# The last 1x1 convolution of a C2f-attention block by one step of Strassen's scheme, and the softmax sums issued one product earlier

## The chip, the cores and the metric

The kernel runs on one core of one Trainium2 chip. Times are device microseconds (us) of an execution. TensorE is called PE in the profile, VectorE DVE, ScalarE ACT; SP and POOL are the two engines that issue the transfers that matter here, each on its own queue (SPq, POOLq).

## The reference

```python
B, C1, C2, N, F, HEADS = 8, 512, 512, 2, 32, 4        # 8 images, 512 channels, 32x32 pixels; C = 256
def L0(x):                                            # on group-normalised x
    t = cbs(x, cv1_w, cv1_bn, 0)                      # 1x1 conv, batch norm, SiLU
    ys = [t[:, :C], t[:, C:]]
    for i in range(N):
        yi = ys[-1]
        z = cbs(yi, m_cv1_w[i], m_cv1_bn[i], 1)       # 3x3 convolution
        z = bot_attention(z, m_qkv_w[i], m_rw[i], m_rh[i])
        z = silu(bn_eval(conv2d(z, m_cv2_w[i], 0), m_cv2_bn[i]))   # "m2" in the kernel
        ys.append(yi + z)
    return cbs(concatenate(ys, axis=1), cv2_w, cv2_bn, 0)          # cv2: 1024 -> 512 channels
out = x + L0(group_norm(x))
```

For one image cv2 is a product of a 512 x 1024 matrix (weights) with a 1024 x 1024 one (channels by pixels). Everything is float32.

## The kernel before

One program handles the eight images in a row. The parts that matter: cv2, the loop of the attention, and what stands around both.

```python
def cv2(b, w2, ys, begun=None, parts={}):
    def residual(oc, half):                            # 256 KB of x, by the POOL queue
        t = act.tile([P, HALF], F32, tag="xr", name="x_res", bufs=2)
        nc.gpsimd.dma_start(t, rows_of(x, oc, half))
        return t
    pieces = [(oc, half) for oc in range(NO) for half in range(NH)]
    res = [residual(*pieces[0]), residual(*pieces[1])]
    for i, (oc, half) in enumerate(pieces):
        if half == 0:
            ...                                        # ps = 16 matmuls of this output chunk
        t = act.tile([P, HALF], F32, tag="t", name="t", bufs=2)
        silu(t, ps[:, half, :], bn_cv2 + oc)           # ScalarE
        nc.vector.tensor_tensor(t, t, res.pop(0), ALU.add)
        q.dma_start(rows_of(out, oc, half), t)         # q is the POOL queue
        if i + 2 < len(pieces):
            res.append(residual(*pieces[i + 2]))

for i in range(len(pairs) + 1):                        # the attention: logits one step ahead of v
    ...
    if i > 0:
        times_v(pairs[i - 1])
        g, j0 = pairs[i - 1][0]
        if j0 == 0:
            if g > 0:
                s_drams[g - 1] = sums(g - 1)
            with tc.issue_after(added.ins):
                behind.get(g, lambda: None)()          # loads, or work for PE's gaps

xs = [load_x(act, b + 1, c, NX) for c in range(NX)]    # at the start of image b: x of the next, by the SP queue
```

The softmax sums of a group of heads go through DRAM: `sums` writes a row (`s_dram`), it comes back over 128 partitions (`sums_all`), VectorE takes reciprocals (`rc`), these are written (`r_dram`) and broadcast (`rs`), all by the SP queue. VectorE multiplies `ao` by `rs` one group later.

## Time and profile before

| | before |
|---|---|
| median of 3 runs | 2486.34 us |
| span of the profiled run | 2485.1 us |
| PE busy | 2416.4 us, 97% |
| DVE, ACT busy | 60%, 38% |

The lines that carry the bound are in the prediction.

The whole idle time before a row goes to what came last. Take cv2 of the second image, whose PE rows the prediction shows. (The prediction calls it the fourth; the rows follow the fourth m2 of the trace, and each image has two.) There ScalarE is idle for 13.81 us up to the SiLU at 662.95, but PE ended the matmuls of that output chunk only near 660.5 (656.93 + 3.60), so some 2.4 us of it are the output's. Seven rows like this, of 13.8 us each, make up nearly all of the 104.8. The next two pairs of outputs (SiLU at 674.30 and 688.03) are 13.73 us apart, and none of their SiLUs waits for a transfer.

### The profile page before, as it was taken

How to read it: one execution, taken by the hardware profiler on the slowest of the kernel's cores; microseconds unless marked ns; L12 is line 12 of the kernel's file. 1: busy time of each engine (PE TensorE's matmuls, PEld its weight loads, DVE VectorE, ACT ScalarE, POOL GpSimd, SP SyncE). 2: the span in 40 equal slices, each digit the busy share in tenths (PEclk: the TensorE clock that was granted, in tenths of full speed). 3: DMA queues.
4: the chain of work that ended last, by engine and by line, in shares of the span. 5: the costliest groups of instructions: out<-in, count | busy, mean ns of one | idle time of the engine just before them, and what ended most of it. 6: DMA issues, size and time to landing. Idle time of an engine off the chain costs nothing.

```text
span 2485.1 us, 35553 instructions
## 1 busy us (share of the span) xinstructions
PE 2416.4 (97%) x14626; PEld 1198.2 (48%) x14626; DVE 1488.6 (60%) x2482; ACT 939.7 (38%) x1280; POOL 104.9 (4%) x355
## 2 busy tenths in 40 slices
PE   6799999999999999999999999999999999999998
PEld 4436446363463634636355363644536354363533
DVE  7678554766456664666546665566564665636654
ACT  2353522525134251443414334153431525325252
POOL 1000000000100001000010000100001000010001
PEclk9899999999999999999999999999999999999999
DMA  7124014040140402304032030502205021050102
GB/s 235 61 90 157 27 39 170 14 153 10 60 149 15 152 15 85 119 14 153 14 133 76 29 134 15 181 28 77 91 10 203 10 87 43 22 191 14 69 10 65
DMA packets 82203, 200.01 MB, mean 80 GB/s; under 512 B 27889, under 2 KB 37809, under 8 KB 69745
## 3 DMA queue, kind: packets, MB, share of 16 engines
q1 hardware_dynamic: 68080, 152.00, 17.8%
q0 software_dynamic: 11808, 45.62, 5.2%
q8 instruction: 117, 1.92, 0.3%
q14 instruction: 54, 0.43, 0.1%
q10 hardware_dynamic: 2144, 0.03, 0.0%
HBM read 167.74 MB, written 29.88 MB: 80 GB/s over the span
## 4 chain that ended last, share of the span: by engine, by line
PE 86%; DVE 5%; ACT 3%; issue 2%; DMA 0%; POOL 0%; SPq 0%; ACTq 0%; DVEq 0%
PE ps L266 33%; PE av_ps L505 15%; PE l_ps L479 14%; PE c_ps L695 13%; PE v_ps L445 4%; PE m_ps L716 4%; ACT pt L483 3%; PE s_ps L523 1%; DVE ao L513 1%; PE s_ps L541 1%; ACT t L252 1%; DVE acc L491 0%; DVE acc L489 0%; DVE v_in L325 0%; DVE st L368 0%
## 5 line engine op out<-in xcount | busy, mean ns | idle before, releaser
L483 ACT ACTIVATE pt<-l_ps 128x1024 f32<-128x1024 f32 x512 | 495.1, 1023 | 230.7 <-PE l_ps L479 230.7
L491 DVE TENSOR_TENSOR acc<-acc,pt 128x1024 f32<-128x1024 f32 x384 | 469.6, 1223 | 131.8 <-ACT pt L483 108.1
L479 PE MATMUL l_ps<-q,kr 64*64 64x512 f32 x4096 | 488.0, 594 | 8.5 <-ACT pt L483 8.5
L505 PE MATMUL av_ps<-pt,vT 64*64 64x512 f32 x4096 | 486.4, 592 | 9.0 <-DVE ao L513 7.5
L695 PEld LDWEIGHTS c_ps<-v_in,u 128*128 128x128 f32 x2688 | 302.6, 192 | 11.5 <-issue 6.7
L695 PE MATMUL c_ps<-v_in,u 128*128 128x128 f32 x2688 | 303.2, 275 | 4.2 <-DVE v_in L325 4.2
L505 PEld LDWEIGHTS av_ps<-pt,vT 64*64 64x64 f32 x4096 | 153.3, 133 | 306.1 <-issue 222.1
L479 PEld LDWEIGHTS l_ps<-q,kr 64*64 64x64 f32 x4096 | 150.2, 133 | 283.1 <-issue 259.1
L266 PE MATMUL ps<-x,w 128*128 128x512 f32 x512 | 227.8, 601 | 2.2 <-DVE x L401 2.2
L266 PE MATMUL ps<-z,qkv_sb 128*128 128x512 f32 x512 | 229.3, 595 | 0.4
L266 PE MATMUL ps<-ypad,w 128*128 128x512 f32 x512 | 227.8, 594 | 0.6 <-ACT t L252 0.6
L489 DVE TENSOR_TENSOR acc<-pt 128x1024 f32<-128x1024 f32 x64 | 78.4, 1225 | 136.8 <-ACT pt L483 136.8
L266 PEld LDWEIGHTS ps<-x,w 128*128 128x128 f32 x512 | 97.1, 192 | 130.8 <-issue 127.3
L266 PEld LDWEIGHTS ps<-ypad,w 128*128 128x128 f32 x512 | 96.5, 190 | 126.0 <-issue 124.6
L433 DVE TENSOR_TENSOR kr<-ps,rw_sb 128x512 f32<-128x512 f32 x64 | 41.2, 686 | 186.0 <-PE ps L266 186.0
L252 ACT ACTIVATE t<-ps,bh,sh 128x512 f32<-128x512 f32 x58 | 42.7, 775 | 274.6 <-PE ps L266 166.8
L266 PEld LDWEIGHTS ps<-z,qkv_sb 128*128 128x128 f32 x512 | 94.7, 190 | 107.2 <-issue 91.8
L778 DVE TENSOR_TENSOR t<-t,x_res 128x512 f32<-128x512 f32 x64 | 43.8, 690 | 170.2 <-ACT t L252 142.8
L266 PE MATMUL ps<-y,w 128*128 128x512 f32 x256 | 118.0, 599 | 4.1 <-ACT t L252 4.1
L332 ACT COPY m<-c_ps 128x256 f32<-128x256 f32 x96 | 35.5, 369 | 221.2 <-PE c_ps L695 214.7
L266 PE MATMUL ps<-ylast,w 128*128 128x512 f32 x256 | 117.2, 595 | 0.0
L445 PE MATMUL v_ps<-qkv_sb,z 128*128 128x256 f32 x512 | 115.7, 379 | 0.0
(121 smaller groups left out, 1980.9 us busy)
## 6 DMA issues: line engine op xcount, KB each, us to landing
u<-u SPq DMA_DIRECT2D x84, 1024.0 KB
w<-in_cv_w_dram SPq DMA_DIRECT2D x25, 1024.0 KB
x<-in_x_dram SPq DMA_DIRECT2D x32, 512.0 KB
x_res<-in_x_dram POOLq DMA_DIRECT2D x64, 256.0 KB, 3.8
out_dram<-t POOLq DMA_DIRECT2D x62, 256.0 KB, 2.9
u<-u_new POOLq DMA_DIRECT2D x12, 1024.0 KB, 5.4
rs<-r_dram SPq DMA_DIRECT2D x96, 128.0 KB
raw<-in_m_cv_w_dram SPq DMA_DIRECT2D x8, 576.0 KB
```

Source lines behind the costliest of these rows:

```text
L252: return nc.scalar.activation(dst, src, AF.Silu, scale=sh[:, k : k + 1], bias=bh[:, k : k + 1])
L266: nc.tensor.matmul(ps[:, half, :], w_of(k), rhs_of(k, half), start=(k == begin), stop=(k == end))
L433: nc.vector.tensor_tensor(dst, img(ps[:, half, :]), rw, ALU.add)
L445: nc.tensor.matmul(ps[:, at, :], z[:, k, ts(j0 + at, P)], qkv_sb[:, n, k, 2 * C : 3 * C], start=(k == 0), stop=(k == NM - 1),)
L479: nc.tensor.matmul(ps[kh * HD : (kh + 1) * HD, hd, :], kr[r, c, o : o + HD], q[r, c, ts(half, HALF)], start=True, stop=True,)
L483: exp = nc.scalar.activation(pt[:, i], ps, AF.Exp, scale=SCALE)
L489: return nc.vector.tensor_tensor(accs[g], pt[:, 0], pt[:, 1], ALU.add)
L491: ins = nc.vector.tensor_tensor(accs[g], accs[g], pt[:, i], ALU.add)
L505: nc.tensor.matmul(avs[g][hd * HD : (hd + 1) * HD, kh, :], vT[r, j, o : o + HD], pt[r, i, hd, :], start=(j == 0), stop=(j == NJ - 1),)
L695: nc.tensor.matmul(ps[:, row, col, :], us[i][:, k, row, col, :], vs[i][:, k, row, col, :], start=(k == 0), stop=(k == NM - 1),)
L716: nc.tensor.matmul(pss[oc][:, half, :], m2_sb[:, n, k, ts(oc, P)], ao[:, k, ts(half, HALF)], start=(k == 0), stop=(k == NM - 1),)
L778: nc.vector.tensor_tensor(t, t, res.pop(0), ALU.add)
```

## The change

The intent is to take an eighth of cv2's matmuls out in seven of the eight images (the last one keeps the plain form). Weights and inputs are cut in 2 x 2 blocks, and seven products of half size replace eight. The four sums of weight blocks are formed once, in the first image, written to DRAM and read back as `ws` in every image. VectorE forms the sums of inputs (`t_in`) and combines the products (`m1`, `c12`, `u3`, `m5`). Independently, the sums of the attention go ahead of the next group's first product with v.

```diff
+    def load_ws():                  # 4 MB of weight blocks and their sums, by the SP queue
+        ...
+    def make_ws(w2):                # first image only: 4 operations of VectorE, 2 MB written
+        ...
+        nc.vector.tensor_tensor(s1, a21, a22, ALU.add)
+        nc.vector.tensor_tensor(s2, s1, a11, ALU.subtract)
+        nc.vector.tensor_tensor(s3, a11, a21, ALU.subtract)
+        nc.vector.tensor_tensor(s4, a12, s2, ALU.subtract)
+        for w, dst in zip(sums, s_dram2):
+            nc.gpsimd.dma_start(dst, w)
 ...
                 if i > 0:
+                    g, j0 = pairs[i - 1][0]
+                    if j0 == 0 and g > 0:
+                        s_drams[g - 1] = sums(g - 1)
                     times_v(pairs[i - 1])
-                    g, j0 = pairs[i - 1][0]
                     if j0 == 0:
-                        if g > 0:
-                            s_drams[g - 1] = sums(g - 1)
                         with tc.issue_after(added.ins):
 ...
+        def strassen(b, ws, y0, y1):
+            ...                      # part1, part2: m1, m5 begun in the attention's tail, kept in SBUF
+            def spare(ps):
+                t = act.tile([P, 2, HALF], F32, tag="x", name="m_kept", bufs=NX)
+            ...
+            def finish(src):         # SiLU, residual, output, as in cv2: two buffers each
+                for o in range(2):
+                    oc, half = pieces.pop(0)
+                    t = act.tile([P, HALF], F32, tag="t", name="t", bufs=2)
+                    silu(t, src[:, o, :], bn_cv2 + oc)
+                    tt(t, t, res.pop(0), ALU.add)
+                    nc.gpsimd.dma_start(out[b, ts(oc, P), ts(half, HALF)], t)
+                    if len(pieces) >= 2:
+                        res.append(residual(*pieces[1]))
+            def part3(y2, ylast, last):
+                ...
+                finish(ps1)
+                tt(m1, new(s2, t2), m1, ALU.add)
+                c12 = spare(None)
+                tt(c12, ps5, m1, ALU.add)
+                finish(c12)
+                u3 = spare(None)
+                tt(u3, new(s3, t3), m1, ALU.add)
+                tt(m5, m5, u3, ALU.add)
+                finish(m5)
+                tt(u3, u3, new(a22, t4), ALU.subtract)
+                finish(u3)
 ...
+                if b == 0:
+                    make_ws(w2)
+                three = s.strassen(b, load_ws(), y0, y1)
                 for i in range(PAIRS):
                     us[0, i] = load_u(0, 0, i)
```

More of the change, by code (lines that the diff above doesn't have):

```diff
@@ L126, with block @@
     raws = [load_raw(0, 0, 0, "k")]
+    KB, CO = (2 + N) * NM // 2, C2 // 2
+    s_dram2 = [tc.dram_tile([P, 2, KB, CO], F32, name=f"s{i}") for i in range(2)]
+    def load_ws():
+        def block(o, i):
+            return cv2_w[ts(i, KB * P), ts(o, CO)].rearrange("(k p) o -> p k o", p=P)
+        pairs = (
+            (block(0, 0), s_dram2[0][:, 0]), (block(0, 1), s_dram2[0][:, 1]),
+            (s_dram2[1][:, 0], s_dram2[1][:, 1]), (block(1, 1),),
+        )
+        ws = []
+        for i, pair in enumerate(pairs):
+            w = ring([P, 2, KB, CO], f"ws{i}")
+            for j, src in enumerate(pair):
+                nc.sync.dma_start(w[:, j], src)
+                ws.append(w[:, j])
+        return ws
+    def make_ws(w2):
+        (a11, a21), (a12, a22) = ((w[:, :, :CO], w[:, :, CO:]) for w in w2)
+        sums = [ring([P, 2, KB, CO], f"s{i}") for i in range(2)]
+        s1, s4, s2, s3 = (w[:, j] for w in sums for j in range(2))
+        nc.vector.tensor_tensor(s1, a21, a22, ALU.add)
[4 more added lines that the diff above has]
+            nc.gpsimd.dma_start(dst, w)
     w1 = load_w1()
@@ L735, in cv2_products, with side, product @@
             return conv1x1(lambda k: w2[2 * k // nk][:, k % (nk // 2), ts(oc, P)], cat, nk, ks, ps, ends)
+        def side(y, half):
+            if len(y.shape) == 3:
+                return y[:, :, ts(half, HALF)]
+            return y[:, :, 1 + half * ROWS : 1 + (half + 1) * ROWS, :].rearrange("p c h w -> p c (h w)")
+        def product(ps, w, rhs, parts=(0, 1), onto=False):
+            for part in parts:
+                for o in range(2):
+                    for c in range(NM):
+                        k = part * NM + c
+                        nc.tensor.matmul(
+                            ps[:, o, :], w[:, k, ts(o, P)], rhs[part][:, c, :],
+                            start=(k == 0 and not onto), stop=(k == KB - 1),
+                            skip_group_check=onto,
+                        )
@@ new lines, in strassen, with sums_of, part1, part2 @@
+        def strassen(b, ws, y0, y1):
+            a11, s1, a12, s4, s2, s3, a22 = ws
+            tt = nc.vector.tensor_tensor
+            top = [[side(y, half) for y in (y0, y1)] for half in range(2)]
+            kept = {}
+            def sums_of(tag):
+                return act.tile([P, 2, NM, HALF], F32, tag=tag, name="t_in")
+            def spare(ps):
+                t = act.tile([P, 2, HALF], F32, tag="x", name="m_kept", bufs=NX)
+                if ps is not None:
+                    nc.scalar.copy(t, ps)
+                return t
+            def part1():
+                kept["t1"] = t1 = sums_of("q")
+                for part in range(2):
+                    tt(t1[:, part], top[1][part], top[0][part], ALU.subtract)
+                kept["ps1"] = ps = ps_big.tile([P, 2, HALF], F32, tag="big", name="c_1")
+                product(ps, a11, top[0])
+                kept["m1"] = spare(ps)
+            def part2():
+                kept["ps5"] = ps = ps_av.tile([P, 2, HALF], F32, tag="av", name="c_5")
+                t1 = kept["t1"]
+                product(ps, s1, [t1[:, 0], t1[:, 1]])
+                kept["m5"] = spare(ps)
+            def residual(oc, half):
+                t = act.tile([P, HALF], F32, tag="xr", name="x_res", bufs=2)
+                nc.gpsimd.dma_start(t, x[b, ts(oc, P), ts(half, HALF)])
+                return t
+            pieces = [(oc, half) for o, half in ((0, 0), (0, 1), (1, 1), (1, 0)) for oc in (2 * o, 2 * o + 1)]
+            res = []
+            def finish(src):
+                for o in range(2):
+                    oc, half = pieces.pop(0)
[6 more added lines that the diff above has]
+            def part3(y2, ylast, last):
+                bottom = [[side(y, half) for y in (y2, ylast)] for half in range(2)]
+                res.extend(residual(*p) for p in pieces[:2])
+                t1 = kept["t1"]
+                t2, t3 = sums_of("k"), sums_of("z")
+                tt(t2[:, 0], bottom[1][0], t1[:, 0], ALU.subtract)
+                with tc.issue_after(last.ins):
+                    tt(t2[:, 1], bottom[1][1], t1[:, 1], ALU.subtract)
+                    for part in range(2):
+                        tt(t3[:, part], bottom[1][part], top[1][part], ALU.subtract)
+                    t4 = sums_of("q")
+                    for part in range(2):
+                        tt(t4[:, part], t2[:, part], bottom[0][part], ALU.subtract)
+                ps1, ps5, m1, m5 = (kept[k] for k in ("ps1", "ps5", "m1", "m5"))
+                for part in range(2):
+                    product(ps1, a12, bottom[0], [part], onto=True)
+                    product(ps5, s4, bottom[1], [part], onto=True)
+                finish(ps1)
+                def new(w, t):
+                    ps = ps_big.tile([P, 2, HALF], F32, tag="big", name="c_new")
+                    product(ps, w, [t[:, 0], t[:, 1]])
+                    return ps
+                tt(m1, new(s2, t2), m1, ALU.add)
[8 more added lines that the diff above has]
+                finish(u3)
+            return part1, part2, part3
@@ L890, with prepare, ahead @@
         z = s.conv3x3(1, vs, u_of(1))
-        w2 = begun = None
-        def ahead():
+        w2 = begun = three = None
+        def prepare():
             nonlocal w2
             w2 = load_w2()
+        def ahead():
+            nonlocal w2, three
             if more:
+                if b == 0:
+                    make_ws(w2)
+                three = s.strassen(b, load_ws(), y0, y1)
                 for i in range(PAIRS):
                     us[0, i] = load_u(0, 0, i)
+            else:
+                w2 = load_w2()
         def first():
             nonlocal begun
-            begun = s.cv2_products(w2, (y0, y1, y2), 0, range(N * NM))
+            if more:
+                three[0]()
+            else:
+                begun = s.cv2_products(w2, (y0, y1, y2), 0, range(N * NM))
         def second():
-            s.cv2_products(w2, (y0, y1, y2), 0, range(N * NM, (1 + N) * NM), begun)
-        ao, check = s.attention_fast(1, z, (b * N + 1) * NM * NH, {1: ahead, NG: first, NG + 1: second})
+            if more:
+                three[1]()
+            else:
+                s.cv2_products(w2, (y0, y1, y2), 0, range(N * NM, (1 + N) * NM), begun)
+        behind = {1: ahead, NG: first, NG + 1: second}
+        if b == 0:
+            behind[0] = prepare
+        ao, check = s.attention_fast(1, z, (b * N + 1) * NM * NH, behind)
         ylast = act.tile([P, NM, HW], F32, tag="v", name="ylast")
@@ L911 @@
             check()
-            if more:
+        if more:
+            three[2](y2, ylast, last)
+            with tc.issue_after(last.ins):
                 vs = s.tiles_in(y1n)
-        s.cv2(b, w2, (y0, y1, y2, ylast), begun, parts)
+        else:
+            s.cv2(b, w2, (y0, y1, y2, ylast), begun, parts)
         y0 = nxt
```

## The prediction

> **What bounds the kernel now.** I read the page first, busy shares and then the chain that ended last:
>
> ```profile
> PE 2416.4 (97%) x14626; PEld 1198.2 (48%) x14626; DVE 1488.6 (60%) x2482; ACT 939.7 (38%) x1280; POOL 104.9 (4%) x355
> PE 86%; DVE 5%; ACT 3%; issue 2%; DMA 0%; POOL 0%; SPq 0%; ACTq 0%; DVEq 0%
> ```
>
> The matmul engine is the bound almost everywhere: a matmul taken out is time taken out, as long as the work put in its place on VectorE, ScalarE and the queues stays behind the matmuls that remain. So I opened the timeline of the two stages that the change touches. First cv2 in the fourth image, from the end of the m2 projection to the next image's first convolution (start us, us, instruction, idle before it):
>
> ```profile
> 642.24 1.13 PE L266 MATMUL ps<-ylast,w 128*128 128x512 f32 x2
> 643.95 1.12 PE L266 MATMUL ps<-y,w 128*128 128x512 f32 x2 [0.58 <-ACT t L252]
> 644.91 2.74 PE L266 MATMUL ps<-ylast,w 128*128 128x512 f32 x6
> 647.49 2.74 PE L266 MATMUL ps<-y,w 128*128 128x512 f32 x6
> 650.06 7.03 PE L266 MATMUL ps<-ypad,w 128*128 128x512 f32 x16
> 656.93 3.60 PE L266 MATMUL ps<-ylast,w 128*128 128x512 f32 x8
> ...
> 684.40 3.60 PE L266 MATMUL ps<-ylast,w 128*128 128x512 f32 x8
> 687.83 21.60 PE L695 MATMUL c_ps<-v_in,u 128*128 128x128 f32 x192
> ```
>
> Each matmul of the program is two records: the 16 from 650.06 to 656.93 are 8 matmuls, 0.859 us each. There is one hole, where the second output chunk waits for ScalarE to empty m2's accumulator: 642.24 to 687.83 is 45.59 us for 52 matmuls, which need 44.67; 0.9 us is lost. After that cv2 is dense. Then a group boundary of the attention, where the sums (s_ps) now stand behind the first product with v:
>
> ```profile
> 606.96 1.90 PE L479 MATMUL l_ps<-q,kr 64*64 64x512 f32 x16
> 608.68 1.90 PE L505 MATMUL av_ps<-pt,vT 64*64 64x512 f32 x16
> 610.39 1.90 PE L479 MATMUL l_ps<-q,kr 64*64 64x512 f32 x16
> 612.52 1.95 PE L505 MATMUL av_ps<-pt,vT 64*64 64x512 f32 x16 [0.23 <-DVE ao L513]
> 614.40 0.64 PE L523 MATMUL s_ps<-acc,ones 128*32 128x256 f32 x8
> 614.97 1.95 PE L479 MATMUL l_ps<-q,kr 64*64 64x512 f32 x16
> ```
>
> Start to start a block takes 1.72 us; at the boundary 2.13, because the single av accumulator is still being emptied by VectorE.
>
> **What the Trainium skill says.** "FP8 and Floating Point Precision", TensorE Precision Notes: a true fp32 product takes four passes through the array. 4 x 512 columns at the 2.4 GHz of "TensorE: Matmul & The Clock Gate" is 853 ns, and the trace has 859: the eight-to-seven saving is real array time. The latter page, The mechanism, says that matmuls are strictly in order; that is why a waiting av product holds up sums whose inputs are ready, and the two rows above agree. "VectorE: DVE Perf Modes", The TRN2 errata, gives (N+151)/0.96 ns for an fp32 tensor_tensor: 1224 ns for 1024 elements; the trace has 1223 to 1225. "DMA: Bandwidth & Descriptors", Queues, rings and completion order: descriptors are consumed in ring order, so a small transfer issued behind large ones on the same queue waits for them. No row of before shows that clearly; my largest cost below rests on it.
>
> **The change part by part.** *Products.* Per image 7 x 8 = 56 matmuls in place of 64: 8 x 0.859 = 6.87 us, in seven images 48.1 us. All were on PE's path.
>
> *The hole after m2.* In the compiled order of the changed kernel m2 is followed by 8 matmuls on y2 into the two accumulators already open, 6.9 us of work that needs neither ylast nor a free accumulator. The 0.9 us should go: 7 x 0.9 = 6.4 us.
>
> *Sums first.* The sums' inputs are ready (the last accumulation of a group ends some 2 us before the boundary), so they fill the wait. Boundary with wait: 610.39 to 614.97, 4.58 us; one without (at 581.01) takes 4.12. The trace's waits count 31 such boundaries of 48: 31 x 0.46 = 14.3 us.
>
> *Added on VectorE*: per image 13 operations on 128x1024, about 1.14 us start to start, 14.8 us in all. Three (t1, and half of t2) stand before the evacuation of the last av accumulator. In before, that evacuation ends 2.4 to 3.4 us ahead of the last sums' matmuls; three operations (3.4 us) bring it to at most 1.0 us behind their start, and the next product starts 1.0 us after it: just in time. The other ten fall into the cv2 stage. I laid them out by hand from m2's end (t = 0), in compiled order: ylast until 3.3, t3, t2, t4 until 9.0, then the convolution's input transform between combinations, the addition for m1 at 21.8 (its product ends at 20.6), c12 to 24.5, u3 at 28.5 (27.5), the last subtraction at 34.6 (34.4). PE's 40 matmuls end at t = 34.4. The next convolution's first output is then drained near 39 rather than 38.6; PE needs its accumulator at 34.4 + 10.7 = 45.1. So VectorE is some 6 us from stopping PE, and I book nothing but 3 us over seven images for just-in-time misses.
>
> *Added on ScalarE*: two copies of about 1 us, behind products, nothing booked.
>
> *The first image* forms the four weight sums (4 x 1.2 us on VectorE, from about 284), writes 2 MB to DRAM through the POOL queue and reads it back through SP's. The compiled SP order puts the broadcast of the first group's reciprocals behind these reads and one load of u. In before:
>
> ```profile
> 288.26 0.32 SPq L569 DMA_DIRECT2D r_dram<-rc  x1
> 289.70 1.13 SPq L571 DMA_DIRECT2D rs<-r_dram  x2
> 294.51 0.69 DVE L579 TENSOR_TENSOR ao<-ao,rs 128x512 f32<-128x512 f32 x1
> 295.12 0.68 DVE L513 TENSOR_TENSOR ao<-av_ps,ao 128x512 f32<-128x512 f32 x1
> ```
>
> In the changed kernel the sums end near 288.6, the second write lands near 296 (the page's 5.4 us to landing for 1 MB by POOL, then 3 more), the broadcast is issued near 297, behind 2 to 2.5 MB still moving; at the 365 GB/s of the second row below this is 6 to 7 us: landing near 304 to 307 instead of before 294.5. The scaling stands ahead of the av evacuation on VectorE, so PE waits: 9 to 11 us, with up to 2 us for a cooled clock (first row: after 8 us of idle PE in the first image its granted clock, the column before the DMA share, was 0.50 for a while). I book 11 us, once.
>
> ```profile
> 66.00:70.00 4.00, 1.08 (x3) 0.79 (x4) 2.45 (x7) 3.79 (x8) 0.00 (x0) 0.50 0.00 0
> 690.00:700.00 10.00, 10.00 (x92) 10.00 (x91) 6.03 (x18) 1.12 (x3) 1.99 (x4) 1.00 0.99 365
> ```
>
> Sum: 2486.3 - 48.1 - 6.4 - 14.3 + 3 + 11 = 2431.5 us, 2.2% less.
>
> **The rivals.** (1) *VectorE becomes the bound of the cv2 stage.* For: some 36 us of work in 34.4, the transform needed by the next convolution shares the in-order engine, and the last output combinations wait for residuals and for two output buffers whose transfers (2.9 and 3.8 us to landing) now compete with image and u loads. Against: the input transform has the whole stage and its last piece ends at 30 against 41.5 when needed, and the convolution tolerates 6 us. Were each image to lose 3 us: 2450. (2) *The first image's round trip costs nothing*, if the small broadcast overtakes the bulk: 2421. (3) *The sums gain nothing*, because the boundary waits for the av evacuation anyway or because changing tile shapes between logits and sums costs what the wait did: 2445. (4) *A ring conflict*: the weights now take four of five ring slots, so two of the next convolution's u loads wait for products. Against: the second is free at t = 14, 27 us before its use; next to no effect.
>
> **Range and chances.** Two per cent is 2436.6, only 5 us above the sum, and the costs are less certain than the savings: the 48 us are arithmetic, the first image's stall could be 4 to 15 us and the tails 0 to 15. I predict 2431, between 2419 and 2445 eight times in ten; faster by over 2% 0.67, within 2% 0.32, slower 0.01.
>
> **What would show it.** Right: from the end of m2 to the convolution 34.4 us dense where 45.6 stood; the boundary at 4.1 us with no wait of av for ao; one wait of about 10 us for ao after a broadcast in the first image's second attention. Wrong: gaps in front of the convolution's matmuls or its copies with VectorE as releaser (rival 1); no wait in the first image (rival 2); boundaries still at 4.6 (rival 3). If PE waits for t_in or ws, my layout by hand is wrong.

## More of the kernel before

A row is line, engine, operation, output<-inputs, shapes, count | busy us, mean ns | idle us of the engine just ahead, with what ended it.

```profile
L778 DVE TENSOR_TENSOR t<-t,x_res 128x512 f32<-128x512 f32 x64 | 43.8, 690 | 170.2 <-ACT t L252 142.8 <-DMA x_res<-in_x_dram 27.4
L252 ACT ACTIVATE t<-ps,bh,sh 128x512 f32<-128x512 f32 x58 | 42.7, 775 | 274.6 <-PE ps L266 166.8 <-DMA out_dram<-t 104.8 <-DVE t L778 3.0
```

In all, ScalarE stood idle 104.8 us before SiLUs that the landing of an output released, and VectorE 27.4 us before additions that a residual released. Neither stopped PE, so the waits cost nothing here.

How long the two transfers take, issue to landing (median us over the whole run, last column):

```profile
x_res<-in_x_dram POOLq DMA_DIRECT2D x64, 256.0 KB, 3.8
out_dram<-t POOLq DMA_DIRECT2D x62, 256.0 KB, 2.9
```

## The result and the profile after

Measured on one chip, four runs each: before 2486.54 us (2485.52 to 2487.82), after **2465.82 us** (2465.57 to 2467.74), ratio 0.9918 with a 95% interval of 0.9901 to 0.9935. Ratios are the mean time of one kernel's fast runs over that of the other's of the same rounds, so they are not quite the ratio of the medians quoted. The change gains 0.8%, not 2.2%: the time lies within 2% of before and outside the predicted range.

The page after, busy shares and chain:

```profile
PE 2375.2 (96%) x14514; PEld 1191.5 (48%) x14514; DVE 1593.3 (65%) x2577; ACT 949.5 (39%) x1294; POOL 105.8 (4%) x357
PE 71%; DVE 14%; DMA 6%; issue 3%; ACT 2%; POOL 1%; SPq 0%; DVEq 0%; ACTq 0%; POOLq 0%
```

PE's share of the chain fell from 86% to 71%, and transfers, which had none of it, have 6%. To see where, I added up stages from the start times of PE's rows. "From m2" means from its start; a second attention reaches from its first projection to the start of m2. The last column is the fastest run, to which I come at the end.

| stage, sum over the images | before | after | difference | fastest run |
|---|---|---|---|---|
| from m2 to the next image's convolution, 7 images | 367.5 | 288.4 | -79.1 | 288.4 |
| that convolution, 7 images | 150.1 | 175.9 | **+25.8** | 150.1 |
| second attention, first image | 90.9 | 110.8 | **+19.9** | 95.2 |
| second attention, the six others | 545.1 | 560.9 | +15.8 | 560.5 |
| first attention and second convolution, 6 images | 822.1 | 820.8 | -1.3 | 818.8 |
| all else | 509.4 | 507.6 | -1.8 | 509.3 |

In each of seven images 3.43 us of products moved from the first row into a second attention (rows 3 and 4), so the first row's true gain is 79.1 - 24.0 = 55.1 us, against 54.5 predicted. The losses are rows 2 and 3.

*Row 2.* PE in the second image, from m2's end (656.07) on; columns are start us, us, row, and in brackets the idle time and its releaser:

```profile
656.07 7.03 PE L786 MATMUL c<-ypad,ws 128*128 128x512 f32 x16
...
669.80 20.76 PE L786 MATMUL c_new<-t_in,ws 128*128 128x512 f32 x48
690.40 10.88 PE L731 MATMUL c_ps<-v_in,u 128*128 128x128 f32 x96
704.47 12.58 PE L731 MATMUL c_ps<-v_in,u 128*128 128x128 f32 x96 [3.19 <-ACT m L368]
```

cv2 is dense as predicted: 656.07 to 690.40 is 34.33 us. The convolution is cut in two by 3.19 us, and its second half takes 12.58 us where the first takes 10.88. The windows view gives the reason for the latter (length, busy us and counts of PE, PEld, DVE, ACT, POOL, then granted clock, DMA share, GB/s):

```profile
705.00:710.00 5.00, 5.00 (x33) 5.00 (x32) 4.93 (x14) 0.00 (x0) 0.00 (x0) 0.66 1.02 402
```

The clock was 0.66 for these 5 us. The convolution's 26.49 us are 5.05 more than 21.44: 3.2 of wait and some 1.9 of cold clock. PE waited for ScalarE and VectorE to empty its first accumulator. What they did instead, VectorE first, then ScalarE, then the SP queue:

```profile
696.92 0.69 DVE L836 TENSOR_TENSOR t<-t,x_res 128x512 f32<-128x512 f32 x1 [4.03 <-DMA x_res<-in_x_dram]
702.35 0.69 DVE L836 TENSOR_TENSOR t<-t,x_res 128x512 f32<-128x512 f32 x1 [4.74 <-DMA x_res<-in_x_dram]
702.96 0.42 DVE L369 TENSOR_TENSOR r_mid<-c_ps,m 128x256 f32<-128x256 f32 x1
```

```profile
695.39 0.81 ACT L288 ACTIVATE t<-m_kept,bh,sh 128x512 f32<-128x512 f32 x1 [5.73 <-DMA out_dram<-t]
698.80 0.81 ACT L288 ACTIVATE t<-m_kept,bh,sh 128x512 f32<-128x512 f32 x1 [2.60 <-DMA out_dram<-t]
```

```profile
684.14 5.88 SPq L104 DMA_DIRECT2D x<-in_x_dram  x3
690.59 3.90 SPq L268 DMA_DIRECT2D u<-u  x2
```

VectorE stands idle for 8.8 us until the last two residuals land, and only then begins to empty the convolution's accumulator (`r_mid`), at 702.96: 46.9 us after m2's end. My layout had the drain done near 39 and gave 45.1 as the limit. ScalarE stands idle for 8.3 us until outputs leave its two buffers; of these, 3.2 us pass before the last subtraction is done (692.89), so 5.1 are the outputs' alone. The two waits are linked: the SiLU before the addition at 696.92 itself ended only at 696.20. Meanwhile the SP queue moves the next image's x and u. The two transfers now take nearly twice as long:

```profile
x_res<-in_x_dram POOLq DMA_DIRECT2D x64, 256.0 KB, 6.9
out_dram<-t POOLq DMA_DIRECT2D x62, 256.0 KB, 5.4
```

and the groups that answer to those of before show who waits for what over the whole run:

```profile
L836 DVE TENSOR_TENSOR t<-t,x_res 128x512 f32<-128x512 f32 x56 | 38.0, 689 | 74.6 <-DMA x_res<-in_x_dram 66.3 <-ACT t L288 8.3
L288 ACT ACTIVATE t<-m_kept,bh,sh 128x512 f32<-128x512 f32 x42 | 33.5, 812 | 189.5 <-DVE m_kept L867 86.8 <-DMA out_dram<-t 60.5 <-DVE m_kept L871 39.2
```

In six images the convolution takes 23.3 to 26.7 us; in the seventh, after which no further x is loaded, 21.44 us. That is the first hint of the cause.

*Row 3.* The first image's second attention, PE and then the SP queue:

```profile
310.32 3.69 PE L541 MATMUL av_ps<-pt,vT 64*64 64x512 f32 x16 [14.39 <-DVE ao L549]
313.79 3.21 PE L515 MATMUL l_ps<-q,kr 64*64 64x512 f32 x16
```

```profile
290.99 0.34 SPq L605 DMA_DIRECT2D r_dram<-rc  x1
...
297.44 0.80 SPq L148 DMA_DIRECT2D ws<-s  x2
298.33 0.38 SPq L268 DMA_DIRECT2D u<-u  x1
298.80 1.14 SPq L607 DMA_DIRECT2D rs<-r_dram  x2
```

The wait is there as predicted, for the broadcast `rs` behind `ws` and `u`, but it is 14.39 us, and the blocks after it take 3.69 and 3.21 instead of 1.90 us: the clock again, which the windows view gives as 0.50 from 310 to 315 us. In all the second attention of this image is 110.84 - 93.37 = 17.5 us longer than those of the other images, not 11.

*The sums.* A boundary after, which fills what was a wait:

```profile
608.65 0.64 PE L559 MATMUL s_ps<-acc,ones 128*32 128x256 f32 x8
609.22 1.95 PE L541 MATMUL av_ps<-pt,vT 64*64 64x512 f32 x16
```

No wait is left. The blocks of logits around it start at 606.82 and 610.99, 4.17 us apart, where 4.58 was.

### The profile page after: what moved, and what is told of

Read it like the earlier page. It is cut to its first block, busy times and chain, and to the rows that moved or that the text cites. A ratio compares the mean times of both kernels' runs of the same rounds, so it can differ in the third digit from the quotient of the medians.

```text
span 2464.4 us, 35583 instructions
## 1 busy us (share of the span) xinstructions
PE 2375.2 (96%) x14514; PEld 1191.5 (48%) x14514; DVE 1593.3 (65%) x2577; ACT 949.5 (39%) x1294; POOL 105.8 (4%) x357
## 4 chain that ended last, share of the span: by engine, by line
PE 71%; DVE 14%; DMA 6%; issue 3%; ACT 2%; POOL 1%; SPq 0%; DVEq 0%; ACTq 0%; POOLq 0%
PE ps L302 17%; PE av_ps L541 17%; PE l_ps L515 17%; PE c_ps L731 7%; PE m_ps L752 4%; PE v_ps L481 4%; DMA x_res<-in_x_dram 4%; PE c L786 3%; DMA rs<-r_dram 1%; PE s_ps L559 1%; DVE acc L527 1%; DVE v_in L361 1%; DVE t L836 1%; DVE t_in L853 1%; DVE t_in L850 1%
## 5 line engine op out<-in xcount | busy, mean ns | idle before, releaser
L731 PE MATMUL c_ps<-v_in,u 128*128 128x128 f32 x2688 | 314.1, 280 | 19.2 <-ACT m L368 16.3
L731 PEld LDWEIGHTS c_ps<-v_in,u 128*128 128x128 f32 x2688 | 312.7, 197 | 27.2 <-ACT m L368 17.2
L786 PE MATMUL c_new<-t_in,ws 128*128 128x512 f32 x336 | 145.3, 592 | 0.0
L752 PE MATMUL m_ps<-ao,m_sb 128*128 128x512 f32 x256 | 112.5, 592 | 0.0
L481 PEld LDWEIGHTS v_ps<-qkv_sb,z 128*128 128x128 f32 x512 | 97.2, 190 | 27.5 <-issue 15.9
L288 ACT ACTIVATE t<-m_kept,bh,sh 128x512 f32<-128x512 f32 x42 | 33.5, 812 | 189.5 <-DVE m_kept L867 86.8
L786 PEld LDWEIGHTS c_new<-t_in,ws 128*128 128x128 f32 x336 | 63.8, 190 | 80.4 <-issue 77.0
L288 ACT ACTIVATE z<-z,bh,sh 128x512 f32<-128x512 f32 x64 | 48.6, 807 | 120.2 <-DVE z L397 120.2
```

What stands on the lines that cost most here:

```text
L288: return nc.scalar.activation(dst, src, AF.Silu, scale=sh[:, k : k + 1], bias=bh[:, k : k + 1])
L481: nc.tensor.matmul(ps[:, at, :], z[:, k, ts(j0 + at, P)], qkv_sb[:, n, k, 2 * C : 3 * C], start=(k == 0), stop=(k == NM - 1),)
L731: nc.tensor.matmul(ps[:, row, col, :], us[i][:, k, row, col, :], vs[i][:, k, row, col, :], start=(k == 0), stop=(k == NM - 1),)
L752: nc.tensor.matmul(pss[oc][:, half, :], m2_sb[:, n, k, ts(oc, P)], ao[:, k, ts(half, HALF)], start=(k == 0), stop=(k == NM - 1),)
L786: nc.tensor.matmul(ps[:, o, :], w[:, k, ts(o, P)], rhs[part][:, c, :], start=(k == 0 and not onto), stop=(k == KB - 1), skip_group_check=onto,
```

## The experiments

**Theory 1**: VectorE's added work fits. What stops PE in row 2 are the residual and output transfers, slowed by the x (and u) loads, through two buffers each and in-order engines. **Theory 2**, the rival: thirteen added operations are too much for VectorE in this stage. **Theory 3**: the first image's loss comes from the queue order alone, the broadcast behind the reading back.

### The parts alone

Only the sums, in the kernel before (the hunk of the attention loop above, nothing else):

> The kernel before, with only the sums moved ahead of the next group's first product with v. My prediction booked 14.3 us for this (31 boundaries of 0.46 us): 2472. The trace of the changed kernel says that the boundaries of which the group-norm matmul is a part keep most of their wait, and that 47 of them together lost 10.0 us: 2476.5 us, ratio 0.996. If the sums gain nothing by themselves (rival 3 of the prediction): 2486.

Measured 2474.22 us against 2487.31, ratio 0.9951 (0.9937 to 0.9964): **-12.2 us**. By stage this is 0.92 us in each second attention and on average some 0.6 in each first one with its tail, eight times. In the trace of this run the boundaries that waited go from 4.57 to 4.16 us in the second attentions, but only from 4.89 to 4.59 in the first ones, where a small product of the next image's group norm stands in the boundary; those that did not wait go from 4.11 to 4.16.

Only Strassen, in the changed kernel:

```diff
-                    if j0 == 0 and g > 0:
-                        s_drams[g - 1] = sums(g - 1)
                     times_v(pairs[i - 1])
                     if j0 == 0:
+                        if g > 0:
+                            s_drams[g - 1] = sums(g - 1)
```

> The changed kernel with only the sums put back behind the next group's first product with v: Strassen alone. If the parts add, it is 10 us slower than the changed kernel (2465.8): 2476, and the start of the next image's convolution (24.3 us too long in six of seven images) and the stall of the first image stay as they are. If the sums ahead of the product made the stall of the first image worse (everything behind the late broadcast), less than 10 us are lost: 2470 or under.

Measured 2480.89 us, ratio 0.9977 (0.9963 to 0.999): Strassen alone gains 6 us, and the two losses stay (convolutions 172.6 us, first image's second attention 113.20). It is 15 us slower than the changed kernel, 3 more than the sums are worth alone; I did not trace those 3 to one place.

### The convolution's stall

The next image's x loaded later, behind u and w1:

```diff
-        if more:
-            xs = [load_x(act, b + 1, c, NX) for c in range(NX)]
 ...
             if g == 0:
                 w1 = load_w1() if more else load_w2(1)
+                if more:
+                    with tc.issue_after(w1_last[0].ins):
+                        xs = [load_x(act, b + 1, c, NX) for c in range(NX)]
+                    norm = s.group_norm(xs)
```

> The changed kernel, but the next image's x is loaded behind the last loads of u and of w1 instead of at the start of the cv2 stage, so nothing but u moves beside the residuals and outputs of cv2. Theory 1 (the residual and output transfers take twice as long beside the x loads, VectorE and ScalarE wait for them in order, and the next convolution's first output is drained late): the convolution's first block is back to about 21.5 us in six images as it is in the seventh, where no x is loaded: up to 25 us less, 2441, unless the later x makes the next cv1 wait, which the group of waits for x would show. Theory 2 (the thirteen added operations are too much work for VectorE in this stage): no change, 2466.

Measured 2450.15 us, ratio 0.985 (0.9837 to 0.9864). The convolutions are back: 151.0 us for seven, 21.44 in five. Behind cv2 of the second image:

```profile
688.07 21.60 PE L733 MATMUL c_ps<-v_in,u 128*128 128x128 f32 x192
```

VectorE's work is unchanged (1593.0 us), so theory 2 falls as the explanation of this stall. Some of the gain is given back in the first attention (826.9 against 820.8 us for six images). Over the whole run the two transfers are still slower than before the change:

```profile
x_res<-in_x_dram POOLq DMA_DIRECT2D x64, 256.0 KB, 5.6
out_dram<-t POOLq DMA_DIRECT2D x62, 256.0 KB, 5.2
```

So x is only part of what slows them. It is the part that counts: in the second image the last two residuals take 6.9 and 9.6 us to land after the change, 5.6 and 5.4 with the late x. The rest comes from u or from the closer spacing of the transfers themselves; no run separates these.

Four residual buffers, x where it was:

```diff
-                t = act.tile([P, HALF], F32, tag="xr", name="x_res", bufs=2)
+                t = act.tile([P, HALF], F32, tag="xr", name="x_res", bufs=4)
-                    if len(pieces) >= 2:
-                        res.append(residual(*pieces[1]))
+                    if len(pieces) >= 4:
+                        res.append(residual(*pieces[3]))
-                res.extend(residual(*p) for p in pieces[:2])
+                res.extend(residual(*p) for p in pieces[:4])
```

> The changed kernel with four buffers for the residual of cv2 instead of two, so that four of its loads stand ahead of their additions; the x loads stay where they were. The run with the later x has shown that the x loads make the six stalls of the next convolution. If what they delay is the residual alone (VectorE waited 4.0 and 4.7 us for it in one image), this takes most of the 25.8 us away: about 2443. If the two output buffers are as bad (ScalarE waited 5.7 and 2.6 us for them), the waits move to ScalarE and less than half is gained: 2455 to 2466. If VectorE's work were the bound: 2466.

Measured 2449.52 us, ratio 0.9849 (0.9836 to 0.9862), between the two outcomes named. VectorE's group now reads:

```profile
L836 DVE TENSOR_TENSOR t<-t,x_res 128x512 f32<-128x512 f32 x56 | 38.0, 688 | 51.4 <-ACT t L288 51.4
```

It waits for no residual any more, but 51.4 us for ScalarE, which still waits 52.1 us for outputs to leave. The convolutions take 151.5 us; the first attention that follows pays 8.2 us more (829.0). The residual transfers are as slow as ever (6.8 us): depth, not speed, made the difference.

The same with results written in place, so that only the first two outputs use the two output buffers:

```diff
-            def finish(src):
+            def finish(src, place=None):
-                    t = act.tile([P, HALF], F32, tag="t", name="t", bufs=2)
+                    t = act.tile([P, HALF], F32, tag="t", name="t", bufs=2) if place is None else place[:, o, :]
-                finish(c12)
+                finish(c12, c12)
```

(and so for `m5` and `u3`)

> As the run with four residual buffers, and in addition SiLU and the residual's addition write in place into the six tiles of combinations that have their own buffers, so that only the first two outputs use the two output buffers. Theory 1 (waits for the residual and for output buffers, not VectorE's work): the convolution's first block is back at 21.4 us in all images, 2465.8 - 25.8 = 2440. Theory 2 (VectorE's work): 2466. A third outcome: the buffers are shared with the next image's x, whose loads then wait for the outputs to land; if that makes the next cv1 or its group norm late, the gain is partly given back and shows in the first attention of the next image.

Measured 2437.62 us, ratio 0.9802 (0.9788 to 0.9815): 28 us less than after. All seven convolutions take 21.43 or 21.44 us, the first attention 818.5 in all.

```profile
L836 DVE TENSOR_TENSOR m_kept<-m_kept,x_res 128x512 f32<-128x512 f32 x42 | 29.0, 691 | 12.5 <-ACT m_kept L288 12.3
```

The residual transfers are no faster than after (6.9 us), and in these groups VectorE and ScalarE wait for no transfer any more. One caution: x shares buffers with these tiles, so its loads also moved some us later here; that alone cannot be the cause of the gain over the run with four residual buffers, whose convolutions were already right, but the share of the x timing in this run is not separated.

### Is VectorE near the bound?

The prediction said that VectorE is some 6 us from stopping PE. Needless operations ahead of the last subtraction, on the in-place kernel:

```diff
-                tt(u3, u3, new(a22, t4), ALU.subtract)
+                last_ps = new(a22, t4)
+                for _ in range(4):                     # 8 in the other run
+                    tt(m1, u3, last_ps, ALU.subtract)
+                tt(u3, u3, last_ps, ALU.subtract)
```

> The run with in-place results (2437.6 us), with four needless copies of the last subtraction ahead of it on VectorE, into a buffer that is free by then: 4 x 1.14 = 4.6 us of VectorE's work at the tightest place of the cv2 stage, in seven images. My prediction said that VectorE is some 6 us from stopping TensorE (39 against 45.1): then 4.6 us more cost nothing in the convolution: 2437.6, at most 1 us per image more from later inputs to the next projection, 2445. If VectorE's work bounds the stage (theory 2), each image loses 4.6 us: 2470.

> The same with eight needless operations, 9.1 us per image: 3 us beyond the slack of 6 us, so about 3 us in each of seven images and some cooled clock: 2437.6 + 21 to 30 = 2459 to 2468. If the slack were much smaller, 2437.6 + 7 x 9.1 = 2501; if much larger, 2438.

Four: 2437.63 us, ratio 0.9798 (0.9784 to 0.9811), the same as without them. Eight: 2467.23 us, ratio 0.9926 (0.9912 to 0.9939), 29.6 us more. In the second image with eight:

```profile
689.60 7.31 PE L731 MATMUL c_ps<-v_in,u 128*128 128x128 f32 x64
699.60 16.16 PE L731 MATMUL c_ps<-v_in,u 128*128 128x128 f32 x128 [2.70 <-issue]
```

A wait of 2.7 us, near 9.1 - 6, and a cold clock on top: the convolution takes 26.00 us. So the slack of VectorE's work is real and lies between 4.6 and 9.1 us, by the size of the wait close to the 6 of my layout (some of the needless operations were compiled in between the drain's, so the 2.7 is not a clean subtraction). Theory 2 is refuted for the changed kernel, and would be right with 8 operations more.

### The first image

Order alone: the reading back issued behind the broadcast.

```diff
+                with tc.issue_after(rs_last[0].ins) if b == 0 else ExitStack():
+                    three = s.strassen(b, load_ws(), y0, y1)
+                    for i in range(PAIRS):
+                        us[0, i] = load_u(0, 0, i)
 ...
+            behind = {0: prepare, 1: lambda: make_ws(w2), 2: ahead, NG: first, NG + 1: second}
```

The text says that the sums are formed one group later. The edit does not do that: `make_ws` stays with the second group, and the two writes are issued at 287.47 and 288.73 us, as after the change (287.42 and 288.68). Only the reading back and the loads of u moved.

> The changed kernel, but in the first image the weight sums are formed one group later and their reading back, with the loads of u behind it, is issued on the sync queue only behind the small broadcast of the first group's reciprocals. If the first image loses its time because that broadcast stands behind some megabytes in the same queue, the wait of 14 us of VectorE for rs in the first image's second attention goes, with the cooled clock after it: about 17 us less, 2449. If the loss were from the writing of the sums to DRAM or from the four additions themselves, it stays at 2466 or moves one group on.

Measured 2462.0 us, ratio 0.99 (0.9885 to 0.9915): 4 us less than after, not 17. The second attention went from 110.84 to 104.66 us. PE waits 5.46 us where it waited 14.39, and 3.15 us one group later, because the second group's small row now stands behind the bulk. Theory 3 holds for part of the loss only; the loss moved one group on, which I had named as the other outcome.

No reading back: the first image multiplies with the blocks and sums where they lie.

```diff
+    def view_ws(w2, sums):
+        a11, a12 = (w[:, :, :CO] for w in w2)
+        s1, s4, s2, s3 = (w[:, j] for w in sums for j in range(2))
+        a22 = ...                                  # 0.5 MB loaded from the weights
+        return [a11, s1, a12, s4, s2, s3, a22[:, 0]]
-                three = s.strassen(b, load_ws(), y0, y1)
+                ws = view_ws(w2, make_ws(w2)) if b == 0 else load_ws()
+                three = s.strassen(b, ws, y0, y1)
```

> The changed kernel, but the first image multiplies with the weight sums and the two weight quarters where they lie, and only the seventh matrix (0.5 MB) is read; the two writes of 2 MB to DRAM for the later images remain. Ordering the broadcast ahead of the reading back gained only 4 us and left waits of 5.4 and 3.2 us: the first group's own small round trip then ran beside the 2 MB of writes, the second group's small write behind the reading. If the reading back causes most of the first image's 17.5 us, 2465.8 - 13 = 2453 or less; if the writes do, one wait of about 5 us stays and 2458 to 2462 results; if neither, 2466.

Measured 2457.62 us, ratio 0.9878 (0.9863 to 0.9893), the middle outcome: attention 101.28 us, one wait of 5.19 us left. With the late x as well:

> First image with the sums where they lie, and the next image's x loaded late: both repairs together. If the two losses are independent, the gains add: 15.7 us of the late x and what the other run of this batch gains, 10 to 15 us: 2435 to 2440, within 2% of the kernel before or just beyond it.

Measured 2442.86 us, ratio 0.9819 (0.9806 to 0.9832). The gains do not quite add: the convolutions keep 5 us of their loss (155.2) and the first attention loses 6. Of the 5 us, 2.4 are in the seventh convolution, beside which no x is loaded, only u; in the run just before, that one lost 1.3. So x is not the whole cause of the stall.

Next I meant to move the 2 MB of writes away from the small round trip as well, once with the conv stall left in and once on the in-place kernel:

```diff
+    def write_ws(sums):                            # called ahead of the first product of cv2
+        with tc.issue_after(rs_last[0].ins):
+            for w, dst in zip(sums, s_dram2):
+                nc.gpsimd.dma_start(dst, w)
```

> The run with the first image's sums where they lie (2457.6 us), and nothing else but the writing of the sums put behind the last broadcast of the first image's second attention. If the wait of 5.1 us for rs that was left there comes from the two writes of 1 MB that run beside the small round trip, the first image's second attention goes from 101.3 to about 93.4 us: 2450. If not: 2457.

> Everything repaired: residuals four deep and results in place as in the run of 2437.6 us, the first image's products with the weight sums where they lie, and the writing of the sums to DRAM put behind the last broadcast of that attention instead of beside the first group's round trip. If the first image's remaining 15.5 us there are the reading back and the writes, and nothing else, 2437.6 - 15.5 = 2422 us, 2.6% under the kernel before, close to 2487.3 - 48.1 - 6.4 - 12.2 = 2420.6, which is the prediction without its two losses. If the writes are not the cause of what was left with the sums in place: about 2429.

Measured 2458.39 us, ratio 0.9889 (0.9873 to 0.9904), and 2428.02 us, ratio 0.9765 (0.9751 to 0.9778). Both fit "the writes are not the cause", and both must not be read so: in the traces the writes are issued at 287.24 and 288.50 us (288.68 and 289.94 in the other run), where they had always been. The compiled order on POOL had not followed the edit. The first run repeats the run with the sums where they lie (2457.62 us), 0.8 us apart; the second combines two repairs that were known. The writes stayed untested, so I asked again with the writes on the SP queue, where the compiled order has them behind the last broadcast, and with additions and writes together moved to the last group:

```diff
-                nc.gpsimd.dma_start(dst, w)
+                nc.sync.dma_start(dst, w)
```

```diff
-            behind[0] = prepare
+            behind = {0: prepare, 3: ahead, NG: first, NG + 1: second}
```

> The run of 2428.0 us with only the writes moved, through the sync queue behind the last broadcast of the first image's second attention, where the compiled order now has them; the four additions stay in the second group. In that group the small write of the reciprocals took 5 us instead of 1.4, and the reciprocal itself ran some 2.5 us later behind the additions. If the writes cause most of the wait: first image's second attention 94 to 96 us and 2421 to 2423. If the additions do: 99 to 101 us and 2426 to 2428.

> The kernel with in-place results and the first image's sums where they lie (the run of 2428.0 us, whose compiled order left the writes beside the first group's round trip), with the four additions and the writes moved from the second group to the last group of that attention, where the products of cv2 that need nothing from the round trip follow. If additions and writes together cause the 7.9 us that the first image's second attention was still too long (101.3 against 93.4), it goes to 93.4 to 96 and the time to 2420 to 2423. If something else in the first image causes it: 2428.

Writes alone moved: **2422.34 us**, ratio 0.9738 (0.9725 to 0.9752). The first image's second attention is 95.16 us, and PE's wait:

```profile
300.71 1.95 PE L553 MATMUL av_ps<-pt,vT 64*64 64x512 f32 x16 [1.69 <-DVE ao L561]
```

The 1.8 us that remain over 93.37 are probably the four additions ahead of the reciprocal: no run took them away alone, but in the next one, where they move too, this boundary takes 4.16 us without a wait. The small write of the reciprocals is followed by its broadcast after 1.84 us (294.06 to 295.90), where with the 2 MB beside it (the first of the two runs above) it took 5.02 us (290.81 to 295.83). Additions and writes in the last group: 2429.62 us, ratio 0.9766 (0.9752 to 0.9779), not the 2420 to 2423 expected. The attention takes 102.07 us: the writes now run beside the third group's small round trip, VectorE waits 7.72 us for that `rs` in order, and what stands behind it, the last sum of exponentials (`acc`) and the emptying of the last accumulator (`ao`), makes PE wait 2.87 and 1.93 us. I had looked at what PE could do in that time and not at what stood behind the wait on VectorE, the same slip as in the convolution.

## Why the prediction was wrong

Summed by its own steps, from the predicted 2431.5 to the measured 2465.8. (One reading was off, without effect on the sum: the rows of "the fourth image" are the second's.)

1. *Products and the hole after m2*: right. 54.5 us predicted, 55.1 measured in the stage; 34.33 us dense.
2. *Sums first*: mechanism right, term of 14.3 us measured 12.2 in the run alone, 2.1 less. I took 4.58 to 4.12, a saving of 0.46 us, for all 31 boundaries. In the run alone it is 0.41 in the second attentions and 0.30 in the first ones, and over the whole run 12.2 / 31 = 0.39.
3. *The tail of cv2*: **this step failed.** "So VectorE is some 6 us from stopping PE, and I book nothing but 3 us over seven images for just-in-time misses." The slack of the work was right (four operations more cost nothing, eight cost 30 us). But the layout held only what VectorE and PE execute; it let every residual and every output buffer be there on time. Measured: 25.8 us instead of 3, 22.8 more. Rival 1 had both halves in one sentence ("the last output combinations wait for residuals and for two output buffers whose transfers (2.9 and 3.8 us to landing) now compete with image and u loads"). Its clause on the transfers was right; its headline, VectorE as the bound, was not. Its 3 us for each image would have been 4.3 in six images (25.8 / 6), and the transfers should have been in the main line: waits for them were visible before in the two groups quoted above (27.4 us for residuals, and of the 104.8 us some 25 for outputs, an estimate from the 2.4 us in each of seven rows and the shorter rows). Before, pairs of outputs come 13.73 us apart, time enough for a late transfer. After, the last two pairs stand close: SiLU of the second pair starts at 680.41, of the third at 687.53, and the last subtraction is done at 692.89, while the x loads start at 684.14.
4. *The first image*: mechanism right, the wait for a broadcast behind the reading back, size wrong: 17.5 us instead of 11, 6.5 more. The broadcast was issued at 298.80 us (I had 297) and landed at 308.97 (I had 304 to 307), and a cooled clock came on top. By the runs the loss falls by 6.2 us with the queue order alone (110.84 to 104.66), 9.6 with no reading back (101.28), and, on the in-place kernel, a further 6.1 with the writes moved (101.26 to 95.16); 1.8 remain. What I had left out is that the 2 MB of writes slow the small transfers of the round trip too, not only the queue they are on.
5. *The rest*: 22.8 + 6.5 + 2.1 - 0.6 = 30.8 of the 34.3 us. What is left, some 3.5 us, lies at least in part in short waits for z and for the next projection's inputs in the first attentions and in two of the second ones (with in-place results the former are 818.5 instead of 820.8). I did not take it apart further.

With every loss mended but those 1.8 us, the kernel needs 2422.34 us. The savings measured or predicted alone, 48.1 + 6.4 + 12.2 from 2487.65, give 2420.9. So the arithmetic of the saving was sound, and most of what was lost was lost to transfers. This version is 2.6% faster than before, and beats both kernels.

On theory 1 the Trainium skill fits, read beforehand and used too narrowly: "DMA: Bandwidth & Descriptors", Queues, rings and completion order, says not only that a ring is served in order (which I used) but that each DMA engine goes round between the queues that have work, a packet at a time. A transfer on the POOL queue then shares the engines with bulk on SP's. The traces agree: 3.8 to 6.9 us for the residual, 2.9 to 5.4 for the output. They show the lengthening, not the turns between packets, nor how much of it is bulk on SP's queue: with the late x, 5.6 and 5.2 us remain.

## What to carry to other kernels

When work moves onto an in-order engine, lay out not its busy time alone but every wait it will stand in, with the landing times of the transfers under the load of that very moment; a wait that is free today can become the cost of whatever is put behind it. When a transfer cannot be made faster, ask for more depth first: here two more residual buffers and results in place were worth 28 us, with residual transfers as slow as in the changed kernel. And when an experiment changes nothing, look in the trace whether the edit reached the program.

## What the Trainium skill lacked or had wrong

- "DMA: Bandwidth & Descriptors" has the order and the turns between queues, but no figure for what bulk on one queue does to a small transfer on another. Here 2 MB of writes on the POOL queue stretched the step from a 4 KB write to the broadcast behind it, on the SP queue, from 1.84 to 5.02 us; bulk ahead in the same queue made the broadcast itself land 10.2 us after issue (298.80 to 308.97).
- "TensorE: Matmul & The Clock Gate", Part 1, puts the cold state after an idle window of about 3.4 us. Waits shorter than that cooled the clock here: after 2.70 us (eight needless operations) and 3.19 us (the changed kernel), both behind cv2 of the second image, the granted clock over about 5 us was 0.66, some 1.9 us more than the wait. It was 0.66 even after 1.90 us (the run with the sums where they lie, at 399.2 us). The length of the wait alone does not decide: the clock stayed at 1.00 after 1.69 us (the fastest run), but also after 2.70 us (eight needless operations, at 404.3 us) and 3.15 us (the run of the queue order, at 321.7 us).
- No page that I read says that a wait on an in-order VectorE or ScalarE without cost becomes one with cost when work for PE is put behind it. Here VectorE was idle 27.4 us before additions that a residual released, at no cost to PE; after the change it was 66.3 us, and the convolutions lost 25.8.
